# The second layer of an MLP by seven quarter products, with whole PSUM tiles in the first layer, and the pointwise convolution and the scores moved

## The chip, the core and the metric

The kernel runs on one core of a Trainium2 chip. The metric is the device time of one execution in microseconds (us). The engines are TensorE (PE; its weight loads are listed as PEld), VectorE (DVE), ScalarE (ACT) and GpSimd (POOL); SyncE (SP) only issues transfers here. Each engine works through its own queue in order and waits for the others by semaphores.

## The reference

Everything is float32. The input is 4 images of 256 channels by 4096 pixels. Two layers follow each other:

```
# layer 0: attention over all 4096 pixels of an image
q, k = wq @ x + bq, wk @ x + bk            # 32 channels each
v    = wv @ x + bv                         # 256 channels
x    = gamma * (v @ softmax(q.T @ k).T) + x
# layer 1
y = x + ls1 * cluster(group_norm(x))       # local clustering of pixels, 256 channels
h = gelu(w1 @ group_norm(y) + b1)          # 256 -> 1024 channels
y = y + ls2 * (w2 @ h + b2)                # 1024 -> 256 channels
z = relu(batch_norm(y * dw))               # per channel
z = relu(batch_norm(wpw @ z))              # pointwise convolution, 256 -> 256
```

The change is about the line with w2, and about what is done beside it.

## The kernel before

**Stages.** The images ("batches" 0 to 3) run one after the other. Each has an attention stage of some 520 us (`weighting`: 64 units of 16 `av` matmuls each, with the scores of a later unit, `score`, between them), the clustering stage (`cluster`) and the MLP stage (`mlp`), of some 250 us. During the MLP stage of batch b the first scores of batch b+1 are already made (`nxt.score`), so that its attention can start at once. One block of batch 2 is left out of its MLP stage and done in the gaps of batch 3 (`late_block`). The order on every engine is the order in which the code issues, written out by hand; nothing is reordered.

**The MLP stage.** It goes over blocks nb of 512 pixels (8 in a batch, 7 in batch 2, so 31 in all), and in each block over four slices j of 128 + 128 hidden channels. One call of `first(nb, j, ...)` is one period. It makes the hidden slice by a scheme of seven products in place of eight: the input's 2 channel halves by 2 pixel halves are the quarters e, f, g, h (t2, t3, t4 are differences made by `norm`), and each product is 128 by 128 by 256 columns. DVE adds the seven results in seven operations (`plus`, L1233) into the four quarters h1 to h4 of the tile `hs`, and ACT applies gelu to each (L1226). `hs` has two buffers, in turn.

**Second layer.** `second` multiplies `hs` by the weights w2: four matmuls of 512 columns per slice (2 halves of the slice by 2 output halves), summed in two PSUM banks `acc`. It is a generator: the matmuls of slice j are issued one by one (`mo`) between the products of slice j+1, to give PE work while DVE and ACT finish a slice. A float32 matmul appears in the trace as two records.

**Around it.** When a block's sums are complete, `finish` (L1277) adds them to y on DVE, and ACT makes z from y (`relu`, L1267, queued in `hooks`). `last` is the pointwise convolution of the block before (four matmuls of 512 columns, `pw`, L1173), issued after slice j = 1; ACT applies the last relu and SP issues two output transfers. Then `norm(nb + 1)` prepares the next block's quarters: two operations on DVE (L1146) and four on POOL (L1159 to L1163). After slice j = 2 a score of the next batch is made: eight matmul records, two ACT copies, and up to four DVE maxima (L372) that wait in the list `maxima` and are taken from it by `rest`, twice in each period. At the end of a batch the maxima are folded into one (`fold`, L389), transposed on PE (`across`, tt, L395) and spread (mb), which the first exponentials of the next batch need.

**Memory.** [...]`ps_s` holds two tiles of two banks (scores, pointwise results and one of the first layer's results, q), `ps_a` the two banks of `acc`, `ps_m` two single banks (u and p of the first layer). In SBUF the tiles of scores, block inputs (`xn2`, read and written by `norm`, `finish`, `last` and the output transfer) and images share one pool of 14 buffers of one size.

**First batch.** Its scores have no MLP stage to lie in. `alone` makes scores 0 to 8 ahead; then `weighting` issues 9 and 10 in unit 0 and one in each unit after that. `derived`, a row of some twenty small DVE and ACT operations with two loads of ACT's tables, follows unit 1.

## Time and profile before

| | |
|---|---|
| median of 3 runs | 3419.7 us (3418.95 to 3419.9) |
| profiled execution | 3419.29 us, its span 3417.5 us |
| PE busy | 3363.0 us (98%) |
| DVE busy | 2069.2 us (61%) |
| ACT busy | 1674.2 us (49%) |
| POOL busy | 1490.3 us (44%) |
| mean granted PE clock | 0.996 |
| first-layer products to end of the MLP stage, batch 0 | 660.0 to 911.8 us |
| in 660 to 912 us: PE, DVE, ACT, POOL busy | 249.0, 131.4, 117.6, 21.7 us |

A line of the profile names the source line, the engine, the operation and out<-in by the program's names, then the shape, the count, the busy time and the mean duration of one. The bracket at the end of a timeline line tells how long the engine had been idle and what ended that. Matmul records overlap, so the rate of PE is the distance between starts. The granted clock is the share of full speed that TensorE was allowed.

### The profile page before, as it was taken

How to read it: one execution, taken by the hardware profiler on the slowest of the kernel's cores; microseconds unless marked ns; L12 is line 12 of the kernel's file. 1: busy time of each engine (PE TensorE's matmuls, PEld its weight loads, DVE VectorE, ACT ScalarE, POOL GpSimd, SP SyncE). 2: the span in 40 equal slices, each digit the busy share in tenths (PEclk: the TensorE clock that was granted, in tenths of full speed). 3: DMA queues.
4: the chain of work that ended last, by engine and by line, in shares of the span. 5: the costliest groups of instructions: out<-in, count | busy, mean ns of one | idle time of the engine just before them, and what ended most of it. 6: DMA issues, size and time to landing. Idle time of an engine off the chain costs nothing.

```text
span 3417.5 us, 31890 instructions
## 1 busy us (share of the span) xinstructions
PE 3363.0 (98%) x11536; PEld 1663.4 (49%) x11536; DVE 2069.2 (61%) x3219; ACT 1674.2 (49%) x2157; POOL 1490.3 (44%) x807
## 2 busy tenths in 40 slices
PE   8999999999999999999999999999999999999999
PEld 4434445665533444565544344466554343445565
DVE  4667764655566766464556676646546766765543
ACT  5555543444555554344455555434446555544444
POOL 2655665210265666521125566652004675672200
PEclk9999999999999999999999999999999999999999
DMA  2000002000000000100000000010000000010000
GB/s 71 13 13 10 16 7 85 7 19 13 19 13 13 13 13 22 70 7 19 19 16 13 10 13 13 22 70 7 19 19 13 13 13 13 13 36 1 13 19 25
DMA packets 41501, 70.01 MB, mean 20 GB/s; under 512 B 9632, under 2 KB 16896, under 8 KB 41344
## 3 DMA queue, kind: packets, MB, share of 16 engines
q1 hardware_dynamic: 36480, 61.16, 5.3%
q10 hardware_dynamic: 4608, 6.30, 0.8%
q8 instruction: 91, 1.49, 0.2%
q0 software_dynamic: 256, 0.52, 0.1%
q14 instruction: 66, 0.54, 0.1%
HBM read 42.68 MB, written 16.89 MB: 17 GB/s over the span
## 4 chain that ended last, share of the span: by engine, by line
PE 95%; DVE 3%; ACT 1%; issue 0%; DMA 0%; SPq 0%; ACTq 0%; DVEq 0%
PE av L473 53%; PE mo L1204 12%; PE sc L359 8%; PE hu L1197 4%; PE pw L1173 3%; PE hp L1197 3%; PE hq L1197 3%; PE vp L310 2%; PE fv L859 2%; PE op L980 1%; PE qp L329 0%; PE kp L287 0%; DVE vf L868 0%; DVE hs L1233 0%; PE agg L889 0%
## 5 line engine op out<-in xcount | busy, mean ns | idle before, releaser
L473 PE MATMUL av<-s,v 128*128 128x512 f32 x4096 | 1820.5, 598 | 0.6 <-ACT s L463 0.6
L468 POOL TENSOR_TENSOR acc<-acc,s 128x1024 f32<-128x1024 f32 x448 | 1057.3, 2360 | 543.2 <-ACT s L463 524.4
L473 PEld LDWEIGHTS av<-s,v 128*128 128x128 f32 x4096 | 759.8, 190 | 1045.4 <-issue 1035.4
L463 ACT ACTIVATE s<-s 128x1024 f32<-128x1024 f32 x512 | 540.1, 1057 | 592.7 <-DVE s L460 549.7
L460 DVE TENSOR_TENSOR s<-s,mb 128x1024 f32<-128x1024 f32 x512 | 595.5, 1205 | 17.8 <-ACT mb L444 15.9
L1204 PE MATMUL mo<-hs,w 128*128 128x512 f32 x992 | 508.3, 595 | 3.8 <-ACT hs L1226 1.6
L381 DVE TENSOR_TENSOR top<-sc,top 128x1024 f32<-128x1024 f32 x196 | 239.4, 1221 | 377.9 <-PE sc L359 377.8
L1226 ACT ACTIVATE hs<-hs,pv_s 128x256 f32<-128x256 f32 x496 | 251.4, 508 | 361.1 <-DVE hs L1233 350.1
L1233 DVE TENSOR_TENSOR hs<-hu,hs 128x256 f32<-128x256 f32 x372 | 157.7, 424 | 356.2 <-ACT hs L1236 205.5
L377 ACT COPY s<-sc 128x1024 f32<-128x1024 f32 x224 | 224.8, 1004 | 228.8 <-PE sc L359 228.8
L1159 POOL TENSOR_TENSOR xn<-xn 128x256 f32<-128x256 f32 x27 | 23.9, 884 | 682.4 <-DVE xn L1146 488.0
L359 PE MATMUL sc<-q,k 32*128 32x512 f32 x2048 | 294.4, 640 | 3.0 <-ACT s L382 3.0
L384 DVE TENSOR_TENSOR top<-sc,top 128x1024 f32<-128x1024 f32 x196 | 240.0, 1224 | 72.6 <-ACT s L377 59.4
L382 ACT COPY s<-sc 128x1024 f32<-128x1024 f32 x224 | 227.0, 1014 | 66.2 <-DVE top L379 36.1
L465 POOL TENSOR_TENSOR acc<-s 128x1024 f32<-128x1024 f32 x32 | 75.3, 2354 | 366.8 <-ACT s L463 366.7
L1233 DVE TENSOR_TENSOR hs<-hq,hs 128x256 f32<-128x256 f32 x372 | 146.3, 421 | 107.5 <-PE hq L1197 103.2
L1204 PEld LDWEIGHTS mo<-hs,w 128*128 128x128 f32 x992 | 186.9, 190 | 42.6 <-ACT hs L1236 7.8
L359 PEld LDWEIGHTS sc<-q,k 32*128 32x128 f32 x2048 | 81.8, 182 | 193.7 <-issue 141.5
L1197 PE MATMUL hp<-xn,w 128*128 128x256 f32 x496 | 150.6, 385 | 2.6 <-ACT v L318 2.6
L1197 PEld LDWEIGHTS hp<-xn,w 128*128 128x128 f32 x496 | 92.4, 190 | 73.0 <-issue 62.5
L310 PE MATMUL vp<-wv_s,x 128*128 128x256 f32 x512 | 123.4, 387 | 0.2 <-ACT v L318 0.2
L1173 PE MATMUL pw<-xn,wpw_s 128*128 128x512 f32 x248 | 112.0, 594 | 3.4 <-ACT xn L1267 2.2
(219 smaller groups left out, 2737.7 us busy)
## 6 DMA issues: line engine op xcount, KB each, us to landing
x<-in_x SPq DMA_DIRECT2D x32, 512.0 KB, 6.6
out<-xn SPq DMA_DIRECT2D x62, 256.0 KB, 2.1
w<-in_w SPq DMA_DIRECT2D x8, 1024.0 KB, 10.2
mr<-row_mx SPq DMA_DIRECT2D x28, 256.0 KB, 3.1
rden<-row_rd SPq DMA_DIRECT2D x28, 256.0 KB, 3.1
q<-q ACTq DMA_DIRECT2D x96, 64.0 KB, 2.0
mix<-in_wfv SPq DMA_DIRECT2D x8, 192.0 KB, 8.1
q<-q SPq DMA_DIRECT2D x24, 64.0 KB, 2.0
```

The lines of the kernel that those rows point to most:

```text
L359: nc.tensor.matmul(halves[r // 2][:, r % 2, :], k_s[rows, g, :], q_s[rows, :], start=True, stop=True)
L381: nc.vector.tensor_tensor(top, halves[1], top, ALU.max)
L382: nc.scalar.copy(s[:, 2:4, :], halves[1])
L384: nc.vector.tensor_tensor(top, halves[0], top, ALU.max)
L460: nc.vector.tensor_tensor(sh, sh, mxs[nb].unsqueeze(1).to_broadcast([P, 2, NB]), ALU.subtract)
L463: nc.scalar.activation(sh, sh, AF.Exp)
L468: nc.gpsimd.tensor_tensor(acc, acc, s[:, 2 * h : 2 * h + 2], ALU.add)
L473: nc.tensor.matmul(av[c], own["v"][:, RG * g + quarter, c * P : (c + 1) * P], slots[u][:, quarter, :], start=(g == 0 and quarter == 0), st ...
L1197: nc.tensor.matmul(out, w[:, j * P : (j + 1) * P], x, start=True, stop=True)
L1204: yield nc.tensor.matmul(acc[c], w2_s[:, jj, c * P : (c + 1) * P], hs[:, i], start=(j == 0 and i == 0), stop=(j == HID // P // 2 - 1 and i ...
L1226: nc.scalar.activation(dst, src, act, bias=bias)
L1233: nc.vector.tensor_tensor(dst, ps, term, ALU.add)
```

## The change

- **Second layer.** In every block but the last of a batch `second_by_seven` takes the place of `second`: per slice seven products of 128 by 128 by 256 columns. The two pixel halves and the two halves of the slice give the quarters h1 to h4 of `hs`, four POOL operations in place make their sums and differences between the products, and the weights are quarters of w2 and three combinations of them. The sums lie in four banks x, y, z, w (two of `ps_a`, two of `ps_m`). `early` takes the first two out as soon as they are complete, `finish` combines the rest with five DVE operations at once and two more given out later by `drips`, one after a `plus`.
- **Weights.** `turn_w2` makes three combinations on POOL before the clustering stage, one of them written over a quarter of w2 (in batch 3 beside it); `mlp` makes the fourth. In the last block the overwritten quarter is loaded again from HBM (256 KB), and the second block of queries (`q_block(1)`), whose buffer a combination takes, is loaded there too.
- **First layer.** Results lie in three two-bank tiles of `ps_s` per slice; u and p no longer use `ps_m`. The product with w_bcd moves from the last place to the fifth. `mo(i)` issues `slots[i]` products of the second layer at four places.
- **Moved.** `last` goes from after j = 1 to after j = 2 (in the last block, into the period of j = 2), the relus of z and the DVE part of `norm` come after j = 1, the POOL part of `norm` behind the POOL operations of the next slice, the score from after j = 2 to after j = 3 with both its copies at once, and `rest` takes one maximum at a time, four times in a block. In batch 0, scores 9 to 15 are spread over (0,2), (1,1), (2,0), (2,3), (3,2), (4,1), (5,0) (unit, quarter). The diagonal of `across` uses another buffer.

```diff
-            half["dg"] = across(0, "rden")
+            half["dg"] = across(0, "t")
...
-            at[0, 2], at[0, 0] = at[0, 0], GRP + 1
+            for i in range(6):
+                del at[i, 0]
+            at.update({divmod(3 * i + 2, RG): GRP + 1 + i for i in range(7)})
...
+    def turn_w2(b, kept):
+
+
+        a11, _, a21, a22 = quarters_w2()
+        w7 = work.tile([P, h_n, P], F32, tag="rden", bufs=1, name=f"w2_7_{b}")
+        nc.gpsimd.tensor_tensor(w7, a21, a11, ALU.subtract)
+        s1 = work.tile([P, h_n, P], F32, tag="q", name=f"w2_1_{b}") if kept else a21
+        nc.gpsimd.tensor_tensor(s1, a21, a22, ALU.subtract)
+        s2 = work.tile([P, h_n, P], F32, tag="q", name=f"w2_2_{b}")
+        nc.gpsimd.tensor_tensor(s2, s1, a11, ALU.subtract)
+        return s1, s2, w7
...
+        w3_s = swap.tile([P, h_n, P], F32, tag="mix", name=f"w2_3_{b}")
+        nc.gpsimd.tensor_tensor(w3_s, s2_s, a12_s, ALU.add)
...
             scaled(0)
-            eng.tensor_tensor(f, f, e, ALU.subtract)
             scaled(1)
-            eng.tensor_tensor(t2, h, f, ALU.subtract)
-            eng.tensor_tensor(t3, e, t2, ALU.subtract)
-            eng.tensor_tensor(t4, t2, g, ALU.subtract)
+
+            def factors():
+                eng.tensor_tensor(f, f, e, ALU.subtract)
+                eng.tensor_tensor(t2, h, f, ALU.subtract)
+                eng.tensor_tensor(t3, e, t2, ALU.subtract)
+                eng.tensor_tensor(t4, t2, g, ALU.subtract)
+
+            return factors
...
-        def last(nb):
+        def last(nb, beside=False):
...
+            if beside:
+                ps = [
+                    ps_m.tile([P, NB], F32, tag="m", name=f"pw{c}_{b}_{nb}") for c in range(KC)
+                ]
+            else:
+                two = ps_s.tile([P, 2, NB], F32, tag="s", name=f"pw_{b}_{nb}")
+                ps = [two[:, c, :] for c in range(KC)]
...
-        norm(0, nc.vector)
+        norm(0, nc.vector)()
         if nxt:
             nxt.q_block(0, nc.sync)
-            nxt.q_block(1, nc.sync)
...
-        def first(nb, j, todo):
+            for i, c in ((0, 0), (1, 0), (1, 1), (0, 1)):
...
+        def second_by_seven(nb, acc, hs, j):
+
+
+            h1, h2, h3, h4 = quarters(hs)
+            one, end = j == 0, j == h_n - 1
+            x, y, z, w = acc
+
+            def q(bank, half, a, t, start=False, stop=False):
+                return nc.tensor.matmul(
+                    bank[:, half * HB : (half + 1) * HB], a[:, j], t, start=start, stop=stop
+                )
+
+            yield q(x, 1, w3_s, h4, one)
+            nc.gpsimd.tensor_tensor(h4, h2, h4, ALU.add)
+            nc.gpsimd.tensor_tensor(h2, h2, h1, ALU.subtract)
+            yield q(x, 0, a12_s, h3, stop=end)
+            yield q(y, 0, a11_s, h1, one, end)
+            nc.gpsimd.tensor_tensor(h1, h1, h4, ALU.subtract)
+            nc.gpsimd.tensor_tensor(h3, h1, h3, ALU.add)
+            if end:
+                early(nb, acc)
+            if behind:
+                behind.pop()()
+            yield q(z, 0, w7_s, h4, one)
+            yield q(z, 1, s1_s, h2, stop=end)
+            yield q(w, 0, s2_s, h1, one)
+            yield q(w, 1, a22_s, h3, stop=end)
+
+        def early(nb, acc):
+
+            yb = block(ys, 0, nb)
+            nc.scalar.copy(quarters(pairs[nb][:, 1])[0], acc[1][:, :HB])
+            nc.vector.scalar_tensor_tensor(yb, acc[0], par("ls2", 0), yb, ALU.mult, ALU.add)
+
+        def first(nb, j, todo, slots, meanwhile=lambda: None):
...
-            u = ps_m.tile([P, NB], F32, tag="m", name=f"hu_{b}_{nb}_{j}")[:, :HB]
-            p = ps_m.tile([P, NB], F32, tag="m", name=f"hp_{b}_{nb}_{j}")[:, :HB]
-            q = ps_s.tile([P, 2, NB], F32, tag="s", name=f"hq_{b}_{nb}_{j}")[:, 0, :HB]
...
+            def banks(n):
+                return ps_s.tile([P, 2, NB], F32, tag="s", name=f"h{n}_{b}_{nb}_{j}")
...
             def plus(dst, ps, term):
                 nc.vector.tensor_tensor(dst, ps, term, ALU.add)
-
-            product(p, W_A, j, e)
+                if drips:
+                    drips.pop(0)()
+
+            def mo(i):
+                for _ in range(slots[i]):
+                    next(todo, None)
...
+            mo(0)
+            ps = banks("p")
+            p, u = ps[:, 0, :HB], ps[:, 1, :HB]
+            product(p, W_A, e)
+            product(u, w_abcd, t2)
             nc.scalar.copy(h1, p)
-            product(u, w_abcd, j, t2)
             plus(h2, u, h1)
-            hook()
-            rest(2 if nb == blocks - 1 and j == 3 else 1)
             mo(1)
-            product(q, W_CD, j, f)
-            product(u, w_bac, j, t3)
+            ps = banks("q")
+            q, u, v = ps[:, 0, :HB], ps[:, 1, :HB], ps[:, 0, HB:]
+            product(q, W_CD, f)
+            product(u, w_bac, t3)
+            product(v, w_bcd, h)
             plus(h3, u, h2)
-            product(p, W_B, j, g)
             plus(h4, q, h3)
+            gelu(h4, h4, hi)
             plus(h2, q, h2)
-            gelu(h4, h4, hi)
+            plus(h2, v, h2)
+            gelu(h2, h2, lo)
+            mo(2)
+            meanwhile()
+            ps = banks("r")
+            p, u = ps[:, 0, :HB], ps[:, 1, :HB]
+            product(p, W_B, g)
+            product(u, W_D, t4)
             plus(h1, p, h1)
             gelu(h1, h1, lo)
-            mo(1)
-            product(u, W_D, j, t4)
             plus(h3, u, h3)
             gelu(h3, h3, hi)
...
-            plus(h2, q, h2)
-            gelu(h2, h2, lo)
-            rest(1)
-            mo(1)
+            mo(3)
...
+            def scaled(y, term, c):
+                nc.vector.scalar_tensor_tensor(y, term, par("ls2", c), y, ALU.mult, ALU.add)
+
+            if len(acc) == KC:
+                for c in range(KC):
+                    scaled(block(ys, c, nb), acc[c], c)
+                    relu(c)
+                return
+
+            _, _, z, w = acc
+            p7, p5, p6, p4 = (t[:, i * HB : (i + 1) * HB] for t in (z, w) for i in range(2))
+            own = pairs[nb][:, 1]
+            d1, d2, d3, d4 = quarters(own)
+            y0, y1 = block(ys, 0, nb), block(ys, 1, nb)
+            nc.vector.tensor_tensor(d4, p6, d1, ALU.add)
+            nc.vector.tensor_tensor(d3, p7, d4, ALU.add)
+            nc.vector.tensor_tensor(d2, p5, d4, ALU.add)
+            scaled(y1[:, HB:], p5, 1)
+            scaled(y1[:, :HB], p4, 1)
+            drips.append(lambda: scaled(y0, own[:, 0], 0))
+            drips.extend([lambda: None] * 2)
+            drips.append(
+                lambda: scaled(
+                    y1.rearrange("p (x n) -> p x n", x=2),
+                    d3.unsqueeze(1).to_broadcast([P, 2, HB]),
+                    1,
+                )
+            )
             for c in range(KC):
-                yb = block(ys, c, nb)
-                nc.vector.scalar_tensor_tensor(
-                    yb, acc[c], par("ls2", c), yb, ALU.mult, ALU.add
-                )
                 hooks.append(lambda c=c: relu(c))
...
+        def rest():
+            if maxima:
                 maxima.pop(0)()
...
-        if blocks == NBLK:
-            at = {(u, 2): u for u in range(GRP)}
-        else:
-            at = {(u, 2): u for u in range(5)} | {(5, 0): 5, (6, 1): 6, (6, 2): 7}
+        acc, todo, slots = None, iter(()), (0,) * 4
+
+        at = {(u, 3): u for u in range(7)} | {(7, 2): 7}
+        if blocks < NBLK:
+            at |= {(6, 1): 6, (6, 2): 7}
+            del at[6, 3]
...
-                hs = first(nb, j, todo)
+                if j == 3:
+                    rest()
+                pw = (lambda: last(nb - 1, True)) if end and j == 2 else lambda: None
+                hs = first(nb, j, todo, slots, pw)
+                if j != 1:
+                    rest()
...
-                if nxt and (nb, j) in at:
-                    nxt.score(at[nb, j], hooks, maxima)
-                if j == 1:
-                    if nb:
-                        last(nb - 1)
+                    if not end:
+                        acc += [
+                            ps_m.tile([P, NB], F32, tag="m", name=f"mo{c}_{b}_{nb}")
+                            for c in range(2, 4)
+                        ]
+                    elif nxt:
+
+                        nc.sync.dma_start(
+                            out=a21_s, in_=w2.rearrange("(k p) m -> p k m", p=P)[:, :h_n, P:]
+                        )
+                        nxt.q_block(1, nc.sync)
+                elif j == 1:
+                    assert not drips
+                    hook()
                     if nb + 1 < blocks:
-                        norm(nb + 1, nc.gpsimd)
-                todo = second(nb, acc, hs, j)
+                        behind.append(norm(nb + 1, nc.gpsimd))
+                elif j == 2 and nb and not end:
+                    last(nb - 1)
+                scored = nxt and (nb, j) in at
+                if scored:
+                    copies = []
+                    nxt.score(at[nb, j], copies, maxima)
+                    copies.pop()()
+                if len(acc) == KC:
+                    todo = second(nb, acc, hs, j)
+                    slots = (2, 1, 1, 0) if scored else (0, 1, 1, 2)
+                else:
+                    todo = second_by_seven(nb, acc, hs, j)
+                    slots = (3, 1, 2, 1) if scored else (0, 2, 2, 3)
...
-            rest(len(maxima))
+            while maxima:
+                rest()
```

## The prediction

> **What bounds the kernel now.** I read the page first (engine shares, then the chain that ended last), then the timeline of one period of the MLP, engine by engine, and last the gaps between matmuls.
>
> ```profile
> PE 3363.0 (98%) x11536; PEld 1663.4 (49%) x11536; DVE 2069.2 (61%) x3219; ACT 1674.2 (49%) x2157; POOL 1490.3 (44%) x807
> PE 95%; DVE 3%; ACT 1%; issue 0%; DMA 0%; SPq 0%; ACTq 0%; DVEq 0%
> L1204 PE MATMUL mo<-hs,w 128*128 128x512 f32 x992 | 508.3, 595 | 3.8 <-ACT hs L1226 1.6
> ```
>
> PE is 98% busy of the 3417.5 us span and carries 95% of the chain: only less PE work, or fewer PE gaps, shortens the span. The second layer (mo, L1204) is 992 records, two for each fp32 matmul. A mean of 595 ns is not what a record costs, since matmuls overlap; the cost is the distance between starts:
>
> ```profile
> 1618.50 0.59 PE L1197 MATMUL hu<-xn,w_abcd 128*128 128x256 f32 x2
> 1618.93 1.02 PE L1204 MATMUL mo<-hs,w 128*128 128x512 f32 x2
> 1619.79 0.59 PE L1197 MATMUL hq<-xn,w 128*128 128x256 f32 x2
> 1620.22 0.59 PE L1197 MATMUL hu<-xn,w_bac 128*128 128x256 f32 x2
> 1620.85 0.42 DVE L1233 TENSOR_TENSOR hs<-hu,hs 128x256 f32<-128x256 f32 x1 [0.45 <-PE hu L1197]
> ...
> 1624.95 0.59 PE L1197 MATMUL hu<-xn,w_abcd 128*128 128x256 f32 x2
> ```
>
> A 512-column matmul moves PE on by 0.86 us (1618.93 to 1619.79), a 256-column product by 0.43 (1619.79 to 1620.22): exactly half. One period (one slice j) is 6.45 us: seven products, 3.01, and four matmuls, 3.44. A product's result is usable on DVE 0.63 us after its start, 0.20 after PE has gone on (1620.22 to 1620.85).
>
> **The change, part by part** (minus is time saved).
>
> *Seven quarter products.* Per period, 4 x 0.86 = 3.44 becomes 7 x 0.431 = 3.02: 0.415 us less. By-seven runs in all blocks but the last of each batch: 31 - 4 = 27 blocks, 108 periods: **-44.8 us**.
>
> Here a rule stands against the row. The Trainium skill's "TensorE: Matmul & The Clock Gate" (Back-to-back issue gap) gives a sustained 81 ns a matmul at 128 columns and 131 at 512, the weight load being part of the price. An estimate on a straight line between them puts 256 columns at 98/131 = 0.75 of 512. Seven products would then cost 7 x 0.75 x 0.86 = 4.5 us a period, 1.07 more than now, +116 us in all. The row shows 0.50 in this very stream, weight loads included, and the added products have the same shape. I take the row.
>
> *Can the four added POOL operations keep up?* I lay one period out, zero at its first product, in the new order: p 0, u 0.43, x1 0.86, x0 1.29, q 1.72, u' 2.15, v 2.58, y 3.01, z0 3.44, r 3.87, r' 4.30, z1 4.73, w0 5.16, w1 5.59, end 6.02. DVE adds (0.42 each, 0.34 apart) run 1.1, 2.8 to 4.25 and 4.5 to 5.4, so the last gelu ends at 6.05; x0 of the next period needs it at 7.31. POOL follows x1 (read at 1.29 + 0.2 + 0.1 of semaphore): h2+h4 1.6 to 2.3, h2-h1 to 3.1; the third operation overwrites h1, so it waits for y: 3.44 + 0.3 = 3.75 to 4.47, the fourth 4.55 to 5.27. w1 wants it at 5.59, z0 wants the first at 3.44. All four fit, with 0.3 us to spare. The POOL durations, 0.72 and 0.80 apart when dependent, are those of the same shape in the norm:
>
> ```profile
> 2523.27 0.88 DVE L372 TENSOR_TENSOR top<-top,s 128x512 f32<-128x512 f32 x1
> 2523.68 1.05 POOL L1161 TENSOR_TENSOR xn<-xn 128x256 f32<-128x256 f32 x1
> 2524.81 0.73 POOL L1162 TENSOR_TENSOR xn<-xn 128x256 f32<-128x256 f32 x1
> 2525.12 0.76 DVE L1233 TENSOR_TENSOR hs<-hq,hs 128x256 f32<-128x256 f32 x2
> ```
>
> Beside DVE's adds, which read PSUM, POOL keeps its 0.73; beside a maximum with both inputs in SBUF it takes 1.05, and DVE 0.88 in place of 0.68. That is the lock of the skill's "SBUF — State Buffer" (SBUF: two separate sides), by which the loser is blocked for the whole operation. The plain durations make the added POOL work free; the lock makes it late where a DVE operation on two SBUF inputs meets the third or fourth POOL operation. Those are the maxima, which run early in a period (no clash), and the two deferred `scaled` of 0.75 us after each block's start, the second at about 4.7, upon the fourth POOL operation. Full blocking delays w1 or the last add by up to 0.6 us, none by 0. I take 0.3 a block, 27 blocks: **+8**. If the cover went in every period, each 0.1 us late would cost 10.8 us.
>
> *Block boundaries and one buffer.*
>
> ```profile
> 1631.41 0.59 PE L1197 MATMUL hu<-xn,w_abcd 128*128 128x256 f32 x2
> 1632.15 1.10 PE L1204 MATMUL mo<-hs,w 128*128 128x512 f32 x2
> ```
>
> The first mo of a block stands 0.31 us after its turn (1631.41 + 0.43), because `finish` still reads the accumulator it overwrites. It recurs at 15 boundaries. `early` now reads that bank a product after its last write: 15 x 0.31 = **-4.7**.
>
> ```profile
> 2519.11 0.59 PE L1197 MATMUL hq<-xn,w 128*128 128x256 f32 x2
> 2522.02 1.00 DVE L1146 TENSOR_SCALAR xn<-x,ga_gn,gb_gn 128x512 f32<-128x512 f32 x2 [7.70 <-DMA out<-xn]
> 2523.41 1.22 PE L1197 MATMUL hu<-xn,w_bac 128*128 128x256 f32 x2 [3.70 <-DVE hs L1233]
> ...
> 2530.40 0.59 PE L1197 MATMUL hp<-xn,w 128*128 128x256 f32 x2
> ```
>
> In batch 2 norm(6) waits for the output DMA of block 4, whose buffer it takes; PE idles 3.86 us and then runs at half clock (the granted clock is 0.93 over 2500 to 2550). From this hq to the next period's hp takes 11.29 us where 4.73 is the rule. In the new order of allocations that tile takes the buffer of block 3, written out a block earlier: **-6.6**. The new pointwise order (after j = 2) puts its two output DMAs 6 us later on SP; the score that now takes block 4's buffer comes some 3 us after they land.
>
> *First period of each batch.* One `u` bank made the w_bac and w_bcd products wait (0.41 + 0.35), and mo waited 0.36 for a gelu. With whole tiles those are gone; x0 then waits about 0.25. The second period's q comes some 1.0 us earlier: 4 x 1.0 = **-4**.
>
> *End of each batch.*
>
> ```profile
> 902.79 1.98 PE L1204 MATMUL mo<-hs,w 128*128 128x512 f32 x4 [0.20 <-ACT hs L1226]
> 902.83 0.69 DVE L389 TENSOR_TENSOR top<-top 128x512 f32<-128x512 f32 x1
> 904.62 0.60 PE L395 MATMUL tt<-ident,top 128*128 128x128 f32 x4
> ```
>
> Now the fold at 902.83 follows one maximum, so the transposes meet no wait, 2.2 us after PE's turn at 902.43. After, `rest` issues one maximum at a time, and DVE's new order has five behind the last add in batches 0 and 1, nine in batch 2 (0.6 us apart). Fold then ends 4.4 and 6.7 us after that turn, PE has two mo to fill 2.6, and the transposes come 2.3 and 4.5 us later than now; behind them wait the diagonal, its broadcast, `exps` and the next batch's first av. Idle of 4 us in batch 2 brings the half clock: the trace's gaps of 2.87, 3.15 and 3.86 us were followed by 3.4 or 6.8 us at half speed, one of 1.9 by none; 1.7 more. The last mo pair waits 0.5 longer in batch 3. 2 x 2.3 + 6.2 + 0.5 = **+11**.
>
> *Scores of batch 0.*
>
> ```profile
> 69.79 1.53 PE L359 MATMUL sc<-q,k 32*128 32x512 f32 x8 [2.99 <-ACT s L382]
> ```
>
> PE waits 3 us here for a score's PSUM, plus 1.7 of half clock. The wider spacing takes this away. But scores 11 and 12 now fall in unit 2, and score 11's copies queue on ACT behind the two table loads of `derived` and exps(3): about 4 us late for score 12, plus the half clock. Bounds -5 and +6; I take **+1.6**.
>
> *At nothing:* w7, s1 and s2 (three POOL operations of 1.27, the row of w_bcd) run in POOL's 26 idle us before the first vf; were it gone, 3.8 us a batch. w3 follows w_bcd, 5 us before its first product. The 256 KB reload of w2's quarter leaves SP after the last z1, has some 7 us, and lands in 3 (the 256 KB mr row) to 6.6 (the 512 KB x row); q_block(1) queues behind it, needed a block later.
>
> Sum: -44.8 + 8 - 4.7 - 6.6 - 4 + 11 + 1.6 = -39.5. The profiled execution took 3419.29 us (1.8 beside the span), 0.4 below the median 3419.7: **3380 us**.
>
> **Rivals.**
>
> 1. *POOL is late in every period.* For: 0.3 us of slack rests on semaphore steps of 0.04 to 0.14 us; two waits per operation. Against: little else runs on POOL here. At 0.2 us a period: 108 x 0.2 = 22, 3402.
> 2. *All of it hides, and the tail is milder.* No clash (-8), half the tail (-5.5), batch 0's start at a gain (-2): 3365.
> 3. *DVE becomes the bound at block boundaries* (slower). It gets five `finish` operations, a maximum and two `scaled` there, about 4 us. By my layout the first add of j = 1 slips 1.4 us, and its PSUM bank is wanted 1.3 us later still. From 1.3 us more lateness PE stalls; at 2.8 more, 27 x 1.5 = 40 eats the gain; an idle near 2.9 us draws the half clock as well: 27 x (2.9 + 1.7) = 124, 3500. Against: DVE is busy 131 of 252 us in this stage.
> 4. *The products stop gaining* (the rule above, or weight loads that wait for POOL and so can't run ahead): +0.4 us a period, about 3420.
>
> **How the numbers follow.** Forecast 0.60, rivals 0.17, 0.15, 0.05 and 0.03. 3380 is the first. 3362 to 3398 takes in the unknown parts (0 to 16 for the clash, -5 to +6 for the start, 3 to 13 for the tail), rival 2 and half of rival 1. A measurement here tells apart about 0.2%, 7 us. Faster 0.93, same 0.02, slower 0.05.
>
> **What would show it.** Right: mid-block periods of 6.02 us without a wait before w1; no gap near 2519; blocks of 29.1 us in place of 30.9; POOL up by some 320 us; transposes late at the three batch ends behind maxima. Wrong: waits of PE on POOL in each period, new half-clock windows within blocks, or 256-column spacing above 216 ns.

## The result, and the profile after

The changed kernel takes 3381.9 us (median of 4 runs, 3377.9 to 3383.5) against 3419.8 (3419.0 to 3421.3) on the same chip: a ratio of 0.9888, 95% interval 0.9876 to 0.9900. The forecast was 3380. The profiled execution took 3380.6 us, its span 3378.8.

From the page of the changed kernel, the engine shares, the chain that ended last, and the second layer's group:

```profile
PE 3320.6 (98%) x12184; PEld 1778.9 (53%) x12184; DVE 2151.6 (64%) x3381; ACT 1659.6 (49%) x2184; POOL 1833.4 (54%) x1255
PE 91%; DVE 7%; ACT 1%; issue 1%; DMA 0%; SPq 0%; ACTq 0%; DVEq 0%
...
L1247 PE MATMUL mo<-hs,w 128*128 128x256 f32 x1512 | 385.9, 381 | 0.0
```

PE is still the bound. The 1512 records are 108 periods of seven matmuls, two records each; 128 records of 512 columns are left for the last blocks. POOL is up by 343 us. What is new is DVE's 7% of the chain (3% before): PE now meets DVE more often just as DVE gets done, or later.

Where the time went is best read in stages, cut at matmuls of the trace: attention from the first to the last av of a batch, clustering from there to the first hp, the MLP from there to the next batch's first av (in batch 3 to the end).

| us | before | after | difference |
|---|---|---|---|
| start to first av | 61.5 | 60.3 | -1.2 |
| attention, batch 0 | 516.8 | 512.8 | -4.0 |
| attention, batches 1 to 3 | 1536.7 | 1536.5 | -0.2 |
| clustering, four batches | 326.0 | 327.9 | +1.9 |
| MLP, batch 0 | 251.81 | 243.70 | -8.1 |
| MLP, batch 1 | 251.81 | 243.69 | -8.1 |
| MLP, batch 2 | 229.73 | 221.12 | -8.6 |
| MLP, batch 3 | 243.09 | 232.81 | -10.3 |
| span | 3417.5 | 3378.8 | -38.6 |

The start (60.3 to 61.7 in the runs below, whatever the kernel) varies without the change. So does clustering (80 to 84 a batch, by where the stretches of half clock fall), but in part it is of the change, as shown below. The MLP stages repeat within 0.01 us from one profile of the changed kernel to the next (243.69, 243.70, 221.11, 232.80 in a second one), so they serve below to tell apart what a median of runs, uncertain by a few us, cannot. Small differences in batches 2 and 3 need care: e4, which leaves the MLP stages alone, is 0.9 off in batch 2 and 0.2 in batch 3. One execution of e3's first run, the profiled one, took 9537.6 us with every matmul slow (an av record 1559 ns, against 598); it stands in no table, and e3 was run a second time.

**A period.** Timeline of the changed kernel in batch 0, from q of one period to q of the next (start, duration, engine, line; the bracket is idle time and what ended it):

```profile
662.34 0.59 PE L1299 MATMUL hq<-xn,w 128*128 128x256 f32 x2
...
664.38 0.73 POOL L1256 TENSOR_TENSOR hs<-hs 128x256 f32<-128x256 f32 x1 [0.67 <-PE mo L1247]
...
665.18 0.73 POOL L1257 TENSOR_TENSOR hs<-hs 128x256 f32<-128x256 f32 x1
...
665.36 1.46 PE L1247 MATMUL mo<-hs,w 128*128 128x256 f32 x6
...
668.38 0.59 PE L1299 MATMUL hq<-xn,w 128*128 128x256 f32 x2
```

6.04 us (6.02 was forecast), in which PE has no wait. The last of the three mo of 665.36 is w1, which needs the POOL operation of 665.18: that ends at 665.91, and w1's turn is 665.36 + 2 x 0.43 = 666.22, 0.31 later.

**A block's second and third period.** Here the forecast saw the deferred `scaled` meet POOL's fourth operation. They do meet, but it is not w1 that pays:

```profile
690.74 0.73 POOL L1257 TENSOR_TENSOR hs<-hs 128x256 f32<-128x256 f32 x1
690.80 1.46 PE L1247 MATMUL mo<-hs,w 128*128 128x256 f32 x6
...
691.12 0.90 DVE L1345 SCALAR_TENSOR_TENSOR x<-xn,pc_s,x 128x512 f32<-128x512 f32 x1
691.95 0.41 DVE L1290 TENSOR_TENSOR hs<-hq,hs 128x256 f32<-128x256 f32 x1
...
692.41 0.70 PE L1299 MATMUL hp<-xn,w 128*128 128x256 f32 x2 [0.15 <-DVE hs L1290]
```

The three mo end their turn at 690.80 + 3 x 0.43 = 692.10, and hp, the first product of the third period, starts at 692.41. It takes the bank of q, whose last reader is the addition of 691.95. That addition stands behind the second `scaled`, and all of DVE's additions of this period stand behind `finish`. The wait of 0.31 us is there in 17 blocks of batches 0 to 2, and with 0.19 to 0.21 in six of batch 3. There the `scaled` is held up longer beside POOL, 1.11 us where 0.74 is its time alone:

```profile
3179.58 0.73 POOL L1257 TENSOR_TENSOR hs<-hs 128x256 f32<-128x256 f32 x1
3179.74 1.11 DVE L1345 SCALAR_TENSOR_TENSOR x<-xn,pc_s,x 128x512 f32<-128x512 f32 x1
...
3181.24 0.70 PE L1299 MATMUL hp<-xn,w 128*128 128x256 f32 x2
```

The second record of the first matmul behind any wait comes 0.10 us late as well (0.70 for the pair at 692.41 where 0.59 is usual), so that each of the 17 costs 0.41. The trace lists no wait of PE for POOL in the changed kernel.

**The end of a batch.** Batch 2:

```profile
2535.81 5.50 DVE L372 TENSOR_TENSOR top<-top,s 128x512 f32<-128x512 f32 x9
2536.16 1.99 PE L1231 MATMUL mo<-hs,w 128*128 128x512 f32 x4 [1.06 <-ACT hs L1287]
...
2541.34 0.69 DVE L389 TENSOR_TENSOR top<-top 128x512 f32<-128x512 f32 x1
2542.09 1.12 PE L395 MATMUL tt<-ident,top 128*128 128x128 f32 x4 [3.95 <-DVE top L389]
2543.00 3.62 PE L1231 MATMUL mo<-hs,w 128*128 128x512 f32 x4
```

Nine maxima stand ahead of the fold, the transposes wait 3.95 us, and the next two mo take 3.62 us where 1.98 is usual: the granted clock is 0.60 and 0.54 in the 8 us from 2540. In batches 0 and 1 the same wait is 1.54 us, and the clock stays full.

**The start of batch 0.** The 2.99 us wait at score 10 is gone; of the scores placed anew, one waits, for 0.45 us:

```profile
70.89 1.14 PE L359 MATMUL sc<-q,k 32*128 32x512 f32 x8
...
77.44 1.28 ACT L463 ACT_TABLE_LOAD   x1
...
82.70 0.99 ACT L377 COPY s<-sc 128x1024 f32<-128x1024 f32 x1
...
84.66 1.47 PE L359 MATMUL sc<-q,k 32*128 32x512 f32 x8 [0.45 <-ACT s L382]
```

**Clustering.** The forecast put `turn_w2` at nothing. Its third POOL operation meets a small operation of the group norm on DVE (L246). Timeline before:

```profile
588.33 0.22 DVE L246 SCALAR_TENSOR_TENSOR mv_gn<-dv_gn,mv_gn 128x1 f32<-128x1 f32 x1
```

and of the changed kernel:

```profile
582.99 1.26 POOL L1134 TENSOR_TENSOR w<-w 128x512 f32<-128x512 f32 x1
583.15 1.11 DVE L246 SCALAR_TENSOR_TENSOR mv_gn<-dv_gn,mv_gn 128x1 f32<-128x1 f32 x1
```

L246 ends together with the POOL operation, and everything that hangs on it is later: the stage's first fv, a long row of matmuls, starts 17.2 us after the last av has ended in batches 0 to 2 and 17.1 in batch 3, where it was 16.5. Of the kernels in the table of experiments, each one with `turn_w2` has 17.1 to 17.3 there, and each one without it (e1, e6, e9) 16.5 to 16.6, as before. So 0.70 us in three batches and 0.59 in the fourth, 2.7 in all, are of the change.

### The profile page after: what moved, and what is told of

Read it like the earlier page. It is cut to its first block, busy times and chain, and to the rows that moved or that the text cites. A ratio compares the mean times of both kernels' runs of the same rounds, so it can differ in the third digit from the quotient of the medians.

```text
span 3378.8 us, 34064 instructions
## 1 busy us (share of the span) xinstructions
PE 3320.6 (98%) x12184; PEld 1778.9 (53%) x12184; DVE 2151.6 (64%) x3381; ACT 1659.6 (49%) x2184; POOL 1833.4 (54%) x1255
## 4 chain that ended last, share of the span: by engine, by line
PE 91%; DVE 7%; ACT 1%; issue 1%; DMA 0%; SPq 0%; ACTq 0%; DVEq 0%
PE av L473 53%; PE sc L359 8%; PE mo L1247 8%; PE hq L1299 4%; PE pw L1206 3%; PE hp L1299 3%; PE hr L1299 3%; PE vp L310 2%; PE fv L857 2%; DVE hs L1290 2%; PE mo L1231 1%; DVE x L1345 1%; DVE top L372 1%; PE op L978 1%; PE qp L329 0%
## 5 line engine op out<-in xcount | busy, mean ns | idle before, releaser
L1287 ACT ACTIVATE hs<-hs,pv_s 128x256 f32<-128x256 f32 x496 | 230.9, 503 | 350.3 <-DVE hs L1290 350.3
L1247 PE MATMUL mo<-hs,w 128*128 128x256 f32 x1512 | 385.9, 381 | 0.0
L1247 PEld LDWEIGHTS mo<-hs,w 128*128 128x128 f32 x1512 | 281.2, 190 | 59.0 <-issue 15.2
L1252 POOL TENSOR_TENSOR hs<-hs 128x256 f32<-128x256 f32 x108 | 78.5, 727 | 305.7 <-PE mo L1247 201.5
L1290 DVE TENSOR_TENSOR hs<-hq,hs 128x256 f32<-128x256 f32 x496 | 198.6, 421 | 68.9 <-PE hq L1299 58.8
L1290 DVE TENSOR_TENSOR hs<-hp,hs 128x256 f32<-128x256 f32 x124 | 52.4, 423 | 267.4 <-ACT hs L1307 267.4
L1299 PE MATMUL hr<-xn,w 128*128 128x256 f32 x496 | 127.5, 379 | 0.3 <-DVE hs L1290 0.3
L1256 POOL TENSOR_TENSOR hs<-hs 128x256 f32<-128x256 f32 x108 | 80.6, 746 | 57.6 <-PE mo L1247 55.7
```

The source lines that it names most:

```text
L1247: return nc.tensor.matmul(bank[:, half * HB : (half + 1) * HB], a[:, j], t, start=start, stop=stop)
L1287: nc.scalar.activation(dst, src, act, bias=bias)
L1290: nc.vector.tensor_tensor(dst, ps, term, ALU.add)
L1299: nc.tensor.matmul(out, w[:, j * P : (j + 1) * P], x, start=True, stop=True)
```

## The experiments

All times are medians; ratios are to the kernel before on the same chip, with 95% intervals.

| kernel | us | ratio | MLP stages, batches 0 to 3 |
|---|---|---|---|
| changed | 3381.9 | 0.9888 (0.9876 to 0.9900) | 243.70, 243.69, 221.12, 232.81 |
| changed, second time | 3383.1 | 0.9894 (0.9878 to 0.9911) | 243.69, 243.70, 221.11, 232.80 |
| e1, by eight everywhere | 3445.8 | 1.0075 (1.0060 to 1.0090) | 263.11, 263.11, 237.55, 241.89 |
| e9, e1 with a maximum moved | 3431.5 | 1.0036 (1.0021 to 1.0052) | 258.88, 258.89, 234.10, 241.87 |
| e5, more POOL work | 3454.8 | 1.0102 (1.0082 to 1.0123) | 260.65, 260.65, 234.90, 255.02 |
| e4, old scores of batch 0 | 3387.1 | 0.9906 (0.9889 to 0.9922) | 243.66, 243.67, 220.23, 233.02 |
| e6, before with one score moved | 3413.4 | 0.9983 (0.9976 to 0.9991) | 251.81, 251.80, 223.95, 243.09 |
| e2, sooner maxima | 3373.7 | 0.9864 (0.9848 to 0.9881) | 241.95, 241.94, 215.00, 232.66 |
| e3, later `scaled` (second run) | 3379.7 | 0.9882 (0.9866 to 0.9899) | 242.84, 242.84, 220.80, 230.82 |
| e7, e2 and e3 | 3367.8 | 0.9848 (0.9834 to 0.9863) | 241.04, 241.05, 214.51, 230.87 |
| e8, e7 and two more | 3363.1 | 0.9835 (0.9820 to 0.9849) | 238.47, 238.48, 212.02, 230.72 |

**e1: the second layer by eight in all blocks.** What do the seven products bring by themselves?

```diff
-                    if not end:
-                        acc += [
-                            ps_m.tile([P, NB], F32, tag="m", name=f"mo{c}_{b}_{nb}")
-                            for c in range(2, 4)
-                        ]
-                    elif nxt:
...
-                        behind.append(norm(nb + 1, nc.gpsimd))
+                        norm(nb + 1, nc.gpsimd)()
...
-            turned = turn_w2(b, not nxt)
+            turned = (None,) * 3
```

> The changed kernel with the second layer by eight quarter products in every block; what only the seven need (the sums of h on POOL, the weight combinations, the reload of w2's quarter, the early reads of an accumulator) goes with them. My theory (PE's stream of matmuls sets the time, a 256-column product moves it by half a 512-column one): each of 27 blocks loses 4 x 0.43 = 1.72 us, 46 in all, less the 0.31 us wait that 24 blocks of the changed kernel have in their third period, plus a 0.31 us wait where the next block's first mo overwrites an accumulator that finish still reads: 46 in all, near 3428. Blocks of 30.8 to 31.1 us in place of 29.4. Rival (whole tiles and the moved pointwise and scores carry a good part of the gain, and the seven products little): no more than 25 us slower, under 3407.

It took 3445.8, 64 us more than the changed kernel and 26 more than the kernel before. The rival is out, and my number was 18 short. In batch 3, where no scores are made, the stage grows by 9.1: seven blocks of 4 x 0.415 = 1.66 are 11.6, less the six waits of 0.2 that went, with what follows them. In batches 0 to 2 it grows by 19.4, 19.4 and 16.4, some 2.8 a block, because of a wait that I had put at 0.31. Chain of waits and timeline of e1, at a block's start:

```profile
PE mo L1229 <- DVE x L1343: 20.5, 20, 1.0
```

```profile
690.21 0.68 DVE L372 TENSOR_TENSOR top<-s 128x512 f32<-128x512 f32 x1
690.81 1.41 DVE L1343 SCALAR_TENSOR_TENSOR x<-mo,pc_s,x 128x512 f32<-128x512 f32 x2
...
691.70 1.10 PE L1229 MATMUL mo<-hs,w 128*128 128x512 f32 x2 [1.03 <-DVE x L1343]
```

The first mo overwrites an accumulator that `finish` (L1343) still reads; 20 waits of 1.03 us, 1.19 from its turn. The changed order puts a maximum ahead of `finish`; in the changed kernel, which reads two banks early and has two more, mo has no such wait.

**e9: e1 with that maximum behind the second period** (it is the order that also ends up in e8).

```diff
-                if j != 1:
+                if j:
                     rest()
```

> The kernel by eight in all blocks, with the maximum that stands ahead of finish in a block's first period moved behind the second period. My theory: the 1.19 us that mo waits at each of 20 boundaries there is finish on DVE, which stands behind a maximum of 0.68 us; it falls by that: 20 x 0.68 = 13.6 us less than by eight with the maximum in its old place, 3432. The rival (finish is late for another reason, as the last products' additions): unchanged within 2 us, 3444 to 3447.

3431.5, 14.3 less: the wait is 8.5 us in 20 places (0.43 each, from 1.03). By MLP stages it is 11.9 less. So 0.60 of the 1.03 us at each boundary is this place in DVE's queue, and the 0.43 that is left is `finish` itself. With 50 us above the changed kernel, the rival of e1 stays out. What by eight and by seven differ in for PE's stream alone is read from batch 3 and from the period: 6.45 to 6.04.

**e5: more POOL work.** How near is w1 to waiting?

```diff
             nc.gpsimd.tensor_tensor(h1, h1, h4, ALU.subtract)
+            extra = work.tile([P, P], F32, tag="extra", bufs=1, name=f"x_{b}_{nb}_{j}")
+            for i in range(2):
+                nc.gpsimd.tensor_tensor(extra, h1[:, i * P : (i + 1) * P], h4[:, :P], ALU.add)
             nc.gpsimd.tensor_tensor(h3, h1, h3, ALU.add)
```

> The changed kernel with two additions of 128 columns on POOL, into a tile that nothing reads, between the third and the fourth POOL operation of each period by seven: some 0.8 us more of POOL a period. My theory (POOL has about 0.3 us to spare before w1 in a period without a score, more in one with): w1 comes 0.5 us late in the 88 periods without a score, about 44 us, 3425, with waits of w1 for POOL. A rival (POOL has a whole microsecond to spare, since w1 is last of its period and PE queues ahead of it): within 5 us of the changed kernel, 3383. Another (POOL is late already in most periods): each of 108 periods grows by the full 0.8, 86 us, 3468.

3454.8, 73 us more, 70 of them in the MLP stages; 44 had been expected. Waits and timeline of e5:

```profile
PE mo L1247 <- POOL hs L1260: 58.1, 88, 1.1
```

```profile
671.42 0.99 POOL L1259 TENSOR_TENSOR x<-hs 128x128 f32<-128x128 f32 x2
...
672.36 0.73 POOL L1260 TENSOR_TENSOR hs<-hs 128x256 f32<-128x256 f32 x1
...
673.14 0.70 PE L1247 MATMUL mo<-hs,w 128*128 128x256 f32 x2 [0.53 <-POOL hs L1260]
```

Exactly the 88 periods without a score wait. The pair takes 0.94 us on POOL's queue (671.42 to 672.36), not 0.8. w1's turn is 671.59 + 2 x 0.43 = 672.45, and it starts 0.69 later (the bracket counts from the end of the matmul before, 0.16 after the turn). So a plain period has 0.94 - 0.69 = 0.25 us to spare: the 0.31 between POOL's end and w1's turn, less the 0.05 that pass from POOL's end to w1's start. In a block's second period w1 is 1.24 late in batches 0 to 2 and 1.01 in batch 3. From their turns the 88 waits are 72 us, with 0.10 behind each 82; some 10 of it take the place of the waits before hp and r that the changed kernel has. The mechanism of rival 1 is real and near: the changed kernel stays clear of it by 0.3 us in a plain period, and by 0.19 in a block's second (691.47 to 690.80 + 2 x 0.43 = 691.66).

**e4: the scores of batch 0 as before.** The forecast and the trace differ in sign here.

```diff
-            for i in range(6):
-                del at[i, 0]
-            at.update({divmod(3 * i + 2, RG): GRP + 1 + i for i in range(7)})
+            at[0, 2], at[0, 0] = at[0, 0], GRP + 1
...
+                if u == 0 and not b:
+                    weigh(u, av, 0)
+                    weigh(u, av, 1)
                 due(u, 0)
```

> The changed kernel with batch 0's scores placed as before the change (the fourth score of the first block ahead of the weighing, the others one a unit). My prediction had the new placement cost 1.6 us, so this run would be 1.6 us faster, with attention of batch 0 at 511. A rival, read from the trace of the changed kernel, where the 3 us wait at the first score is gone and score 12 waits only 0.61: the placement gains all of the 4 us by which batch 0's attention is shorter (516.77 to 512.77), and this run is 4 us slower, attention of batch 0 at 516.8, with the wait near 70 us and a half clock of 3.4 us back.

3387.1, 4 to 5 us more than the changed kernel; attention of batch 0 takes 517.73 in place of 512.77, and the wait is back:

```profile
69.39 2.42 PE L359 MATMUL sc<-q,k 32*128 32x512 f32 x8 [2.99 <-ACT s L382]
```

The pair of the forecast's +1.6 and the measured -4 is settled: the new placement gains.

**e6: the kernel before with one score moved,** so that block 6's tile takes another buffer.

```diff
-            at = {(u, 2): u for u in range(5)} | {(5, 0): 5, (6, 1): 6, (6, 2): 7}
+            at = {(u, 2): u for u in range(6)} | {(6, 1): 6, (6, 2): 7}
```

> The kernel before with one edit: in batch 2 score 5 moves from block 5's first period to its third, behind the allocation of block 6's tile, which then takes the buffer of block 3 in place of block 4's. My theory: norm(6) no longer waits for an output DMA, the 3.86 us gap near 2519 goes and with it the half clock of 6.8 us behind it; the MLP of batch 2 falls from 229.7 to 223.1, 6.6 us less, about 3413. A rival: the maxima of that score, two periods later, are now behind the last addition and put 1 to 3 us on the end of batch 2, or the score itself waits for block 4's output: 4 us or less gained.

3413.4, as forecast (the interval, 0.9976 to 0.9991, excludes no change). Timeline of e6 where the gap of 3.86 us was:

```profile
2518.49 0.59 PE L1197 MATMUL hq<-xn,w 128*128 128x256 f32 x2
...
2518.92 0.59 PE L1197 MATMUL hu<-xn,w_bac 128*128 128x256 f32 x2
```

hu follows hq by 0.43. The stage falls by 5.8, not 6.6: two boundary waits of 0.31, with 0.08 behind each, are there that batch 2 did not have before. A sixth of the whole gain was thus to be had by one line.

**e2: sooner maxima in the last block.**

```diff
-        def rest():
-            if maxima:
+        def rest(n=1):
+            for _ in range(min(n, len(maxima))):
                 maxima.pop(0)()
...
                 if j == 3:
-                    rest()
+                    rest(2 if end else 1)
+                if end and j > 1:
+                    drips.append(lambda: rest(2))
...
-                if j != 1:
-                    rest()
+                rest((1, 3, 2, 1)[j] if end else j != 1)
```

> The changed kernel with the maxima of the last scores drained sooner in the last block of each batch (up to three after the second period, two ahead of the last, two behind its first addition), so that none is left behind the last addition. My theory (the transposes at a batch's end wait for the fold, and the fold for DVE's queue of maxima): the waits before tt, 1.54 us in batches 0 and 1 and 3.95 in batch 2, go, and with the last the half clock of 6.8 us there; 1.7 + 1.7 + 4.1 + 2.5 = 10 us less, about 3372. A rival: the gelus set the end anyway, since mo waits 1.06 us for the last of them just before; then the maxima, pushed between the additions, delay the gelus and the gain is under 4 us, or the half clock stays: 3378.

3373.7, 8 us less than the changed kernel; by stages 1.75, 1.75, 6.12 and 0.15, 9.8 in all. Timeline of e2 at the end of batch 0:

```profile
888.11 0.68 DVE L389 TENSOR_TENSOR top<-top 128x512 f32<-128x512 f32 x1
888.46 1.98 PE L1231 MATMUL mo<-hs,w 128*128 128x512 f32 x4 [1.06 <-ACT hs L1287]
...
890.28 0.60 PE L395 MATMUL tt<-ident,top 128*128 128x128 f32 x4
```

The fold comes straight behind the last additions, tt has no wait in any batch, and batch 2 shows no half clock. The rival's other half is true as well: the 1.06 us wait for the last gelu is untouched.

**e3: the second `scaled` one addition later.**

```diff
-            drips.extend([lambda: None] * 2)
+            drips.extend([lambda: None] * 3)
```

> The changed kernel with one empty step more ahead of the second deferred scaled, so that this 0.75 us operation on DVE follows the last addition that reads q's bank and not the last but one. My theory: the 0.31 us wait of p (0.19 in batch 3) in the third period of a block is that bank, held by the last addition behind finish's operations and the scaled; it goes in 24 blocks, 18 x 0.31 + 6 x 0.19 = 6.7 us less, blocks of 29.1 in place of 29.4 in batches 0 to 2, about 3375. The rival (the wait is for ACT, whose gelus or the score's copies hold the bank): nothing changes within 1 us, or the additions on r come too late and a wait of a few tenths appears before the first products on h of the next period.

3377.4 to 3379.9 us in three executions, without a profile that tells of stages. e7 came next, and then this kernel once more:

> The changed kernel with the second deferred scaled one addition later, once more, for its stages. By the two runs in which this edit stands beside the sooner maxima: the wait of p in the third period goes and one of 0.25 us comes at the first product on h of the same period in batches 0 to 2; MLP stages 243.7 - 0.9, 243.7 - 0.9, 221.1 - 0.5 and 232.8 - 1.8, in all 4 us less than the changed kernel's, 3378 to 3380. The first theory of this edit would have stages of 241.3, 241.3, 219.1 and 231.0.

3379.7, the stages 0.86, 0.85, 0.32 and 1.99 below the changed kernel's, 4.0 in all: the second expectation, and 2.7 short of the first.

**e7: e2 and e3 together.**

> The changed kernel with both edits tried singly: the maxima drained sooner at the batches' ends, and the second deferred scaled behind the last addition that reads q's bank. My theory: beside the first edit alone (MLP stages 241.95, 241.94, 215.00, 232.66) the second takes 6 x 0.31 from each of batches 0 and 1, 5 x 0.31 from batch 2 and 6 x 0.19 from batch 3, with some 0.1 for each wait beyond its length since the first matmul behind a wait takes 0.10 longer: 239.5, 239.5, 213.0, 230.9, and 3364 to 3368. The rival (the bank is held by something else, or the wait only moves to the first product on h of the next period): stages within 0.5 us of the first edit's, 3372 to 3374.

3367.8; beside e2 the stages fall by 0.91, 0.89, 0.49 and 1.79. Both theory and rival hold in part. Timeline of e7 in the place of the wait:

```profile
691.37 0.74 DVE L1345 SCALAR_TENSOR_TENSOR x<-xn,pc_s,x 128x512 f32<-128x512 f32 x1
...
691.89 0.59 PE L1299 MATMUL hp<-xn,w 128*128 128x256 f32 x2
692.02 0.75 DVE L1290 TENSOR_TENSOR hs<-hr,hs 128x256 f32<-128x256 f32 x2
...
692.76 1.38 PE L1247 MATMUL mo<-hs,w 128*128 128x256 f32 x4
...
693.43 0.30 PEld L1247 LDWEIGHTS mo<-hs,w 128*128 128x128 f32 x2 [0.48 <-ACT hs L1287]
```

hp has its turn (the three mo from 690.60 end at 691.89). The additions on r now stand behind the `scaled`, the last gelu is later, and the second mo on h waits 0.25 for it (four records take 1.38, 1.03 is usual). So in batches 0 to 2 the place of the `scaled` decides which of DVE's readers is late, and a good part of the lateness comes from the start of the queue (e8). In batch 3, where no maximum stands ahead of `finish`, the whole of the wait is gone: there the `scaled` takes 0.74 in its new place, 0.37 less than beside POOL, which is more than the wait of 0.2.

**e8: a sooner `finish`, and q sooner at the batch's end.** Beside e7, the last block takes one maximum instead of two behind the first addition of its last period, and:

```diff
-                rest((1, 3, 2, 1)[j] if end else j != 1)
+                rest((1, 3, 2, 1)[j] if end else j != 0)
...
                     slots = (2, 1, 1, 0) if scored else (0, 1, 1, 2)
+                    if scored and j == 2:
+                        slots = (2, 0, 1, 1)
```

> The kernel with both edits (maxima drained sooner at the batches' ends, the second scaled one addition later) and two more: the maximum that stood ahead of finish in a block's first period goes behind the second period, and the last period of batches 0 to 2 gives one matmul of the second layer from ahead of q to behind r. My theory: finish starts 0.68 us sooner on DVE, so that all additions of the second period are sooner and the 0.25 us wait of the first product on h (0.35 with the slower first matmul behind it) goes in the 17 blocks that have it, 6.0 us; q comes 0.86 us sooner at a batch's end and the wait of mo for the last gelu, 1.06 us, falls by some 0.6 three times, 1.9 us: 3367.8 - 7.9 = 3360, MLP stages 238.3, 238.3, 212.1, 230.9. A rival (the maximum now delays the additions of the third period, or norm's operation behind the second): waits of a few tenths turn up one period later, stages within 1 us of 241.0, 241.0, 214.5, and 3366.

With it ran the changed kernel:

> The changed kernel unaltered, beside which the next run is measured on one chip. All theories: 3382 within 3, MLP stages 243.7, 243.7, 221.1, 232.8 (the batch 2 one within 1, since a half clock can fall differently).

3363.1 against 3383.1, 20 us less than the changed kernel, with intervals against the kernel before (0.9820 to 0.9849, 0.9878 to 0.9911) that are well apart; the stages are within 0.2 of those expected, the median 3 us above. Timeline of e8 at a block's second period, and its chain of waits:

```profile
687.85 0.59 PE L1299 MATMUL hp<-xn,w_abcd 128*128 128x256 f32 x2
687.86 0.41 DVE L1358 TENSOR_TENSOR xn<-mo,xn 128x256 f32<-128x256 f32 x1
...
690.09 1.01 DVE L1345 SCALAR_TENSOR_TENSOR x<-xn,pc_s,x 128x512 f32<-128x512 f32 x1
```

```profile
PE mo L1231 <- ACT hs L1287: 0.6, 3, 0.2
```

`finish` (L1358) starts with the second product of the period, 0.01 us after it; in the changed kernel it was 0.61 after it (715.90 and 716.51 in batch 0). The trace lists no wait in a plain block any more, and those for the gelu at three batch ends are down from 3.2 us to 0.6.

## Why the prediction was right, and where it was not

The sum was right to 2 us, in part by luck: the MLP terms were 6.0 us too hopeful, the scores of batch 0 came out 5.6 better than forecast, and 2.7 us in clustering were not foreseen.

**Seven products: right.** 6.04 us a period against 6.45; a 256-column record moves PE by 0.216 us and a 512-column one by 0.429. The -44.8 stands: it is the same count of records by the same spacing. The sustained figures of the skill's "TensorE: Matmul & The Clock Gate" (Back-to-back issue gap), from which the forecast's estimate was +116, do not describe this float32 stream.

**Block boundaries and the clash: right in kind, wrong in place, 3 us too small.** I had -4.7 for the old boundary wait and +8 for `scaled` meeting POOL, +3.3 together. The old waits, 15 of 0.31 with 0.08 behind each, went: -5.8. What came is 17 of 0.31 and six of 0.2 before hp, with 0.10 behind each, two of 0.33 before r and one of 0.25 before hp in the last two blocks of the batches with scores, and 0.08 in one more place a block, whose cause stays open: about +12. Blocks are 29.41 us (30.91 before), not 29.1. The failed step is "Full blocking delays w1 or the last add by up to 0.6 us": w1 starts at its turn, with 0.19 us to spare. POOL's operation starts first, so DVE's `scaled` pays, with 0.90 in place of 0.74 in batches 0 to 2 and 1.11 in batch 3, and it is the last addition on q, and so q's bank, that is late (e3, e7). By these durations the meeting with POOL makes about half of the 0.31 in batches 0 to 2 and all of the wait in batch 3, some 4.5 us of the 12 (17 x 0.16 + 6 x 0.3), an estimate, since no run takes the meeting away alone; the rest comes from `finish` and a maximum at the head of DVE's queue (e8). That is the mechanism of rival 3. The working for it there followed the first addition and its bank, which had 1.3 us to spare; the last addition on q, behind a `scaled`, had none.

**Batch 2's buffer: right.** e6 shows it alone: 6.0 us in the medians, 5.8 in the stage.

**First period of each batch: mis-sized.** The second period's q comes 0.58 us sooner in batches 0 to 2 and 0.67 in batch 3 (6.95 us after the first hp in place of 7.53), not 1.0: -2.4 for -4. Whole tiles end the waits inside the period, but the second period's p needs the bank of q, read by an addition that ends with the period, and waits 0.90 for it.

**Ends of batches: right.** Forecast +11. The wait before tt (1.7 from its turn in batches 0 and 1, 4.1 in batch 2), the wait for the gelu (1.2 against 0.36 before) and the half clock in batch 2 (2.5 more, less 0.7 for a wait before pw that is gone) give 2.6, 2.6 and 6.8; batch 3 has 0.5 less, where 0.5 more was forecast: +11.5. e2 takes 9.8 of it back, by draining the maxima alone.

**Scores of batch 0: wrong sign.** Forecast +1.6, measured -4.0 in the stage, 4 to 5 when it is undone (e4). The gain of the lost wait was right. The failed step is "about 4 us late for score 12, plus the half clock": it waited 0.45, 0.6 from its turn, since score 11's copies began at 82.70, right behind exps(3), and the second table load, at 77.44, was over before those exponentials needed ACT.

**`turn_w2`: put at nothing, measured +2.7.** The failed step is that w7, s1 and s2 "run in POOL's 26 idle us before the first vf". They do, and POOL is free in time, but DVE is not: L246 waits for the third of them, and the first fv with it. e1 and e9, which leave them out, have the old 16.5 us.

MLP terms together: -41.1 forecast, -35.1 measured (the terms above give -35.3). Scores: +1.6 and -4.0. What is left, +0.5, is -1.2 at the start and -0.2 in attention, which no run here ties to the change, and +1.9 in clustering: the +2.7, and -0.8 by where the half clock falls. Rival 1 is excluded for this kernel by the absence of any wait on POOL, rival 4 by the spacing; of rival 2, "all of it hides" falls with 0.41 us at each boundary.

## What to carry to other kernels

When PE work is taken out, each engine that fed PE with a little to spare moves onto the path: follow every reader of a PSUM bank to the last one, not the first, and ask what stands ahead of it in its engine's queue. Work that nobody waits for (here maxima) belongs behind the operations that free banks, and is drained before the operation that needs it all; the four moves of e8 were worth 20 us, half of what the change itself brought. Work on an idle engine is free only if no other engine waits for it meanwhile: the three operations of `turn_w2` ended in time, and cost 2.7 us. A wait that lasts shows at once in the stage times of two traces, which mostly repeat to 0.01 us where medians scatter by 3.

## What the hardware showed beside that

A matmul that starts after a wait costs more than the wait: its second record came 0.10 us late in nearly every such place (0.70 for a pair of 256 columns, 0.59 without), a quarter of the price of a 0.31 us wait.

A DVE operation with both inputs in SBUF that started while a POOL operation ran was held up to POOL's end, all but its first 0.19 us. The `scaled`, 0.74 us by itself, ended 0.55 us after the POOL operation wherever it had started: it took 0.85 with 0.30 of overlap (e5), 0.90 with 0.35 (691.12 in the changed kernel), 1.01 with 0.46 (690.09 in e8), 1.11 with 0.57 (3179.74), and 0.74 with 0.12 (e8). Blocked from its first moment, the one of 691.12 would have taken 1.09. L246, 0.22 us by itself, took 1.11 with 1.10 of overlap. The POOL operation that started first kept its 0.73; one that started 0.49 us after a `scaled` took 0.84. This is the lock of the forecast, but for the start of the operation that waits.

PE's idle time of 1.5 us left the clock full in batches 0 and 1, 3.95 us in batch 2 brought a granted clock of 0.54 to 0.60. In between it was not the same each time. PE is idle for 2.71 us before cnt, a matmul of clustering, in batches 0 to 2: half clock followed in batches 0 and 1 before the change, and in 0 and 2 after it. The forecast read these gaps (2.87 us from PE's turn) as followed by it; one of the three was not.
